# Softmax attention on one core: the bias row built behind the last block's values, three set-up pieces behind the first maxima, and 78 maxima steps ahead of the loop

## The chip, the core and the metric

The kernel runs on one core of a Trainium2 chip, in one launch. A core has five engines that run beside each other and meet at semaphores: TensorE (PE, matrix products and transposes; its weight loads are listed as PEld), VectorE (DVE), ScalarE (ACT), GpSimd (POOL) and SyncE (SP, which here only issues DMAs). The metric is the device time of one execution in microseconds (us); of several runs the median is given.

## The reference, cut to what matters

The input `x` has shape (2, 2048, 256). Four layers follow one another: softmax attention, a gated rotation network ("ffn"), linear attention, and the rotation network again. The change touches the first layer alone:

```python
def _L0_attn_a_ref(x, Wq, bq, Wk, bk, Wv, bv, Wo, bo):   # HIDDEN 256, 16 heads of 16, 4 key/value heads
    q = x @ Wq + bq
    k = x @ Wk + bk
    v = x @ Wv + bv
    ...
    scores = jnp.einsum('bghnd,bhsd->bghns', q, k)
    attn = jax.nn.softmax(scores / SCALE, axis=-1)        # SCALE = 4
    out = jnp.einsum('bghns,bhsd->bghnd', attn, v)
    out = out.transpose(0, 3, 1, 2, 4).reshape(B, N, NUM_HEADS * HEAD_DIM)
    return out @ Wo + bo
...
x = x + _L0_attn_a_ref(_layernorm(x, axis=-1), ...)
x = x + _L0_ffn_ref(_layernorm(x, axis=-1), ...)
x = x + _L0_attn_b_ref(_layernorm(x, axis=-1), ...)
x = x + _L0_ffn_ref(_layernorm(x, axis=-1), ...)
```

## The kernel before, in words

**Blocks and units.** The 4096 tokens are cut into NB = 8 blocks of BLK = 512 tokens, of which blocks 0 to 3 are batch 0 and 4 to 7 batch 1. A *unit* u = (j, g) is one block of queries and one group g of four heads, one for each of the KV = 4 key/value heads r; there are 32 units. Softmax is done with the true maxima, so each score is computed twice: once with queries on the partitions, to find the largest score of each query, and once with keys on the partitions, for the exponentials.

**The maxima.** `largest()` is a generator. One *step* of it is one 128x512 score product `s` on PE (line 376) and one reduction `mx` on DVE (line 380). A unit has 64 steps: 4 blocks of keys, 4 tiles of queries, and the heads r in the order 0, 1, 3, 2. The 16 features of a head are held as high and low parts in 64 rows; head r uses rows 0 to 63 of the array when r is even and rows 64 to 127 when r is odd (`row` in `step`). The products go through a ring of three PSUM banks (`a_s`, tag `s`), so step n cannot write before step n-3 has been reduced. Unit 0 alone also uses banks of the ring `p`. After 64 steps the generator negates and splits the maxima (`nm`, line 390, and `mt`, lines 394 to 398), turns them (`mr`, line 403) and sends them over DRAM to `mrows` (lines 407 and 412). For unit 0 this happens at once; for the units after it the turn is done inside the next unit's first steps, after the step (kb, qi, r) = (0, 0, 2), which is that unit's fourth.

**The first stage.** Before the loop, blocks are normalised (`look`, `spread`), turned (`features`, line 131), and projected to keys (`keys`, 309), queries (`asked`, 336) and values (`values`, 326). What is left of this after the first four steps of the maxima is the generator `pieces()`, 22 pieces long: queries of blocks 1 to 3, then features, keys and two times queries for each of the blocks 4 to 7. The lines 622 to 627 of the kernel before run the steps 4 to 73 (`LEAD` = 74) and put a piece behind certain steps: behind every third one from 4 to 52, then behind 64, 66, 68, 70 and 72. The order of DVE, ACT, POOL and SP in this stage is the order of the program (`in_order`), and PE's is too, up to the first passes of the loop.

**The bias row.** `rows()` is a generator that loads the output weights and the bias `bo` with nine DMAs on SP (lines 216 and 217), multiplies it into a diagonal on POOL (`a_db`, line 221), sums that over partitions with a product on PE (`a_pb`, line 226) and copies the row on DVE (`a_bo_row`, line 227). In the kernel before, POOL's part stands behind the queries of block 3 and ahead of the features of block 4, and the PE and DVE part behind the values of block 4. The row is used first when unit 0 is finished (line 467), in the loop.

**The loop.** There are 32 x 16 = 512 passes, one for each unit u and each 128 keys kb. A pass issues on PE, in this order: two steps of the maxima, `score(0)`, `score(1)`, `shift(0)`, `shift(1)`, `score(2)`, one step, `score(3)`, `shift(2)`, one step, `shift(3)`, and then the four products `av` of the pass before (`weigh`, line 633). `score` is line 648 and `shift`, which adds the negated maxima, line 652; both use rows 0 to 63 for even r and rows 64 to 127 for odd r. ACT takes the exponentials `e` (line 656). In the kernel before, a pass with odd kb among the first twelve (`MORE` = 6) takes one more step at its end. The steps are counted through all units, so that the remainder of the count by four says which heads the steps of a pass belong to; the maxima end 20 passes ahead of the end of the loop.

Of the kernel before, what the change touches and what calls it, by code (L numbers as in the profile page):

```python
# [67 lines left out]
def tile_hybrid(ctx: ExitStack, tc: tile.TileContext, x: bass.AP, consts: bass.AP, wa_d: bass.AP, wf_d: bass.AP, wb_d: bass.AP, out: bass.AP):  # L68
# [84 lines left out]
    def attention_a():  # L153
        with ExitStack() as st:
# [206 lines left out]
            def largest():  # L361


                turning = []
                for u, (j, g) in enumerate(units):
                    k0 = (j // BPB) * N
                    qP = queries[u]
                    mx = sb.tile([P, KV, 4, 4], F32, tag="mx", name=f"mx{u}")
                    first = u == 0

                    def step(kb, qi, r):

                        pool, tag = (psp, "p") if first and (4 * qi + r) % 5 > 2 else (pss, "s")
                        s = pool.tile([P, BLK], F32, tag=tag, name=f"s{u}_{kb}_{qi}_{r}")
                        row = slice(64 * (r % 2), 64 * (r % 2) + 64)
                        mm(  # L376
                            s, qP[r // 2][row, qi * P : (qi + 1) * P],
                            kP[r // 2][row, k0 + kb * BLK : k0 + (kb + 1) * BLK], start=True, stop=True,
                        )
                        nc.vector.tensor_reduce(mx[:, r, qi : qi + 1, kb], s, AX.X, ALU.max)  # L380

                    for kb in range(4):
                        for qi in range(4):
                            for r in (0, 1, 3, 2):
                                step(kb, qi, r)
                                if (kb, qi, r) == (0, 0, 2) and turning:
                                    turning.pop()()
                                yield
                    nm = sb.tile([P, KV, 4], F32, tag="nm", name=f"nm{u}")
                    nc.vector.tensor_reduce(nm, mx, AX.X, ALU.max, negate=True)  # L390

                    mt = sb.tile([P, KV, 2, 4], F32, tag="mt", name=f"mt{u}")
                    if first:
                        nc.vector.tensor_copy(mt[:, :, 0, :].bitcast(F32R), nm)
                        nc.vector.tensor_tensor(mt[:, :, 1, :], nm, mt[:, :, 0, :], ALU.subtract)
                    else:
                        nc.scalar.copy(mt[:, :, 0, :].bitcast(F32R), nm)  # L397
                        nc.gpsimd.tensor_tensor(mt[:, :, 1, :], nm, mt[:, :, 0, :], ALU.subtract)  # L398

                    def turn_maxima(u=u, mt=mt):  # L400

                        mr = sb.tile([P, 32], F32, tag="mr", name=f"mr{u}")
                        turn = nc.vector.transpose(mr, mt.rearrange("p r i q -> p (r i q)"))
                        tc.keep_in_program_order(turn)
                        d = dram.tile([2 * KV, BLK], F32, tag="dm", name=f"dm{u}")
                        for i in range(4):
                            nc.sync.dma_start(
                                d.rearrange("r (q b x) -> (r q) b x", b=4, x=32)[:, i, :], mr[32 * i : 32 * i + 32, :]
                            )
                        for p in range(2):  # L410
                            for i in range(2):
                                nc.sync.dma_start(
                                    mrows[u % 2][p][64 * i : 64 * i + 2, :].bitcast(F32),
                                    d[4 * p + 2 * i : 4 * p + 2 * i + 2, :],
                                )

                    if first or u + 1 == len(units):
                        turn_maxima()
                    else:
                        turning.append(turn_maxima)  # L420
# [83 lines left out]
                        nc.vector.tensor_tensor(pair, pair, po.rearrange("p (t d) -> p t d", t=2), ALU.add)  # L504
                        yield


            LEAD, MORE, WARM = 64 + 10, 6, 6
            ahead = largest()
            begin = len(nc.cur_bb.bb.instructions)  # L510
            loads = ExitStack()
# [81 lines left out]
            def pieces():  # L593

                memsets()
                look(4)
                values(3)
                for j in range(1, BPB):
                    for m in range(2):
                        asked(j, m)  # L600
                        yield
                        if (j, m) == (2, 0):
                            spread(4, ld, 0)
                next(more)
                for j in range(BPB, NB):
                    features(j, ld, 0)
                    if j + 1 < NB:
                        look(j + 1)
                    yield
                    keys(j, ld)()  # L610
                    if j + 1 < NB:
                        spread(j + 1, ld, 0)
                    yield
                    asked(j, 0)
                    yield
                    asked(j, 1)
                    values(j)
                    if j == BPB:
                        next(more)
                    yield  # L620

            rest = pieces()
            for n in range(4, LEAD):
                next(ahead)
                if (n % 3 == 1 and n < 55) or (n > 63 and n % 2 == 0):
                    next(rest, None)
            in_order(begin, (engines.DVE, engines.Activation, engines.Pool, engines.SP))

# [9 lines left out]
            for u, kb in ((u, kb) for u in range(len(units)) for kb in range(KB)):  # L638
                if (u, kb) == (0, 4):
                    in_order(begin, (engines.PE,))  # L640
                qP, mrow = queries[u], mrows[u % 2]
                k0 = units[u][0] // BPB * N + kb * P
                t, es = [], []

                def score(r):
                    row = slice(64 * (r % 2), 64 * (r % 2) + 64)
                    t.append(psp.tile([P, BLK], F32, tag="p", name=f"p{u}_{kb}_{r}"))
                    mm(t[r], kP[r // 2][row, k0 : k0 + P], qP[r // 2][row, :], start=True, stop=False)  # L648

                def shift(r):  # L650
                    row = slice(64 * (r % 2), 64 * (r % 2) + 64)
                    mm(t[r], pick[row, :], mrow[r // 2][row, :], start=False, stop=True)  # L652

                def exp(r):
                    es.append(sb.tile([P, BLK], F32, tag="e", name=f"e{u}_{kb}_{r}", bufs=8))
                    nc.scalar.activation(es[r], t[r], AF.Exp, scale=1.0 / HD**0.5)  # L656


                next(ahead, None)
                next(ahead, None)  # L660
                score(0)
                score(1)
                shift(0)
                shift(1)
                exp(0)
                exp(1)
                if kb == 1:
                    next(done, None)
                score(2)
                next(ahead, None)  # L670
                score(3)
                shift(2)
                next(ahead, None)
                shift(3)
                exp(2)
                exp(3)
                if last is not None:
                    if last[1] == 0:
                        av = pav.tile([P, BLK], F32, tag="av", name=f"av{last[0]}")
                    weigh(*last)  # L680
                    if last[1] == KB - 1:
                        done = finish(last[0], av)
                last = u, kb, es
                if kb > 1:
                    next(done, None)
                    next(norms, None)
                if kb % 2 == 1 and u * KB + kb < 2 * MORE:
                    next(ahead)
                if u % G == 1 and kb == 1 and G < u < 4 * G:
                    norms = norm(u // G - 1)  # L690
                if kb == 4 and u + 2 < len(units):
                    project(u + 2)()
                if rest is not None and next(rest, "end") == "end":
                    rest = None
                    loads.close()
                    late = later_pools["late"] = ctx.enter_context(tc.tile_pool(name="late", bufs=1, side="right"))
                    for n, (name, of) in enumerate((("wf", wf_d), ("wb", wb_d))):
                        weights[name] = late.tile([P, of.shape[1]], F32, name=name)
                        nc.sync.dma_start(weights[name], of)
                    for name in ("w4", "b3"):  # L700
                        at = slice(*_WF[name])
                        nc.sync.dma_start(weights["wf"][64:P, at], wf_d[0:64, at])
# [826 lines left out]
```

## Time and profile before

| What | Value |
|---|---|
| Time, median of 3 runs | 2137.04 us (2135.6 to 2137.55) |
| The profiled execution | 2140.99 us, span 2139.2 us |
| PE busy | 2109.2 us (99%) |
| DVE busy | 1701.3 us (80%) |
| ACT busy | 1428.9 us (67%) |
| POOL busy | 355.6 us (17%) |
| Mean granted PE clock | 0.990 |
| `mx` on DVE, 2048 times | 1272.2 us, mean 683 ns |
| `e` on ACT, 2048 times | 1057.7 us, mean 603 ns |
| First score of the loop on PE | 106.78 us |
| Last step of the maxima begins on PE | 1481.31 us |

The span is the time from the first to the last instruction of the core; the execution's own time lies 1.8 us above it. Busy PE time holds matrix products that overlap: two products in different halves of the rows run beside each other, and the mean of one (471 ns for `s`) contains its latency. Idle time of an engine is put down to the instruction that released it. The granted clock is what the throttle let through to PE, 1.00 or 0.50 in every row of this profile that lies between two changes.

### The profile page before, as it was taken

What the parts mean: (1) busy time and instruction counts of PE and PEld (TensorE: products, weight loads), DVE (VectorE), ACT (ScalarE), POOL (GpSimd) and SP (SyncE); (2) the same over time, 40 slices, a digit from 0 to 9 for tenths busy, and PEclk for the clock granted to TensorE, in tenths of its full rate; (3) what the DMA queues carried; (4) which work ended last, traced back from release to release, by engine and by line L of the source; (5) the groups of instructions that cost most, each with busy time, mean ns of one, the idle gap of its engine ahead of it and who ended that gap; (6) DMA issues with size and microseconds to landing.
All of it is one profiled execution on the core that took longest, in us unless ns stands there. A gap on an engine that the chain in (4) does not pass through costs nothing.

```text
span 2139.2 us, 38744 instructions
## 1 busy us (share of the span) xinstructions
PE 2109.2 (99%) x14158; PEld 1018.1 (48%) x14158; DVE 1701.3 (80%) x3241; ACT 1428.9 (67%) x2787; POOL 355.6 (17%) x352
## 2 busy tenths in 40 slices
PE   9899999999999999999999999999999999999998
PEld 4344444444444444444444444444443567676434
DVE  7699998998998999899899899986134688876335
ACT  4377777776777877777777777778864445454443
POOL 3100000000001000000000000000145345541450
PEclk9799999999999999999999999999999999999999
DMA  6320110101101011010110101100100000000002
GB/s 207 88 87 10 49 37 17 47 10 47 39 17 37 19 47 39 17 48 10 46 39 17 44 12 47 39 17 8 52 0 1 1 1 1 2 1 2 0 0 79
DMA packets 59695, 68.71 MB, mean 32 GB/s; under 512 B 24944, under 2 KB 34032, under 8 KB 59248
## 3 DMA queue, kind: packets, MB, share of 16 engines
q1 hardware_dynamic: 58592, 64.79, 11.1%
q8 instruction: 111, 1.82, 0.3%
q10 hardware_dynamic: 720, 0.92, 0.1%
q14 instruction: 80, 0.66, 0.1%
q0 software_dynamic: 192, 0.52, 0.1%
HBM read 35.78 MB, written 26.21 MB: 29 GB/s over the span
## 4 chain that ended last, share of the span: by engine, by line
PE 93%; DVE 3%; issue 1%; ACT 1%; POOL 1%; DMA 1%; SPq 0%; DVEq 0%; POOLq 0%; ACTq 0%
PE av L633 24%; PE s L376 22%; PE p L648 11%; PE q1f L817 8%; PE p L652 7%; PE q2f L827 4%; PE pe L1114 2%; PE bpo L1140 1%; PE po L499 1%; PE pq L975 1%; PE pv L984 1%; PE pw L984 1%; PE pk L975 1%; PE q3f L839 1%; DVE mx L380 1%
## 5 line engine op out<-in xcount | busy, mean ns | idle before, releaser
L380 DVE TENSOR_REDUCE mx<-s 128x1 f32<-128x512 f32 x2048 | 1272.2, 683 | 111.9 <-PE s L376 106.2
L656 ACT ACTIVATE e<-p 128x512 f32<-128x512 f32 x2048 | 1057.7, 603 | 313.5 <-PE p L652 306.5
L376 PE MATMUL s<-a_kP,qP 64*128 64x512 f32 x2048 | 707.0, 471 | 4.9 <-DVE mx L380 3.0
L652 PE MATMUL p<-a_m,a_pick 64*128 64x512 f32 x2048 | 587.4, 415 | 0.0
L376 PEld LDWEIGHTS s<-a_kP,qP 64*128 64x128 f32 x2048 | 283.6, 184 | 569.6 <-DVE mx L380 553.1
L633 PE MATMUL av<-e,a_v 128*32 128x512 f32 x4096 | 546.8, 605 | 0.0
L648 PE MATMUL p<-qP,a_kP 64*128 64x512 f32 x2048 | 526.7, 394 | 2.6 <-ACT e L656 2.6
L648 PEld LDWEIGHTS p<-qP,a_kP 64*128 64x128 f32 x2048 | 286.9, 185 | 64.2 <-ACT e L656 25.4
L652 PEld LDWEIGHTS p<-a_m,a_pick 64*128 64x128 f32 x2048 | 284.2, 184 | 26.3
L817 PE MATMUL q1f<-zq,wf 128*128 128x512 f32 x384 | 175.6, 600 | 0.0
L633 PEld LDWEIGHTS av<-e,a_v 128*32 128x32 f32 x4096 | 81.0, 108 | 129.6 <-issue 121.5
L818 ACT ACTIVATE a1f<-q1f,wf 128x512 f32<-128x512 f32 x96 | 65.8, 686 | 102.8 <-PE q1f L817 99.4
L398 POOL TENSOR_TENSOR mt<-nm,mt 128x16 f32<-128x16 f32 x31 | 6.9, 221 | 737.3 <-ACT mt L397 737.3
L817 PEld LDWEIGHTS q1f<-zq,wf 128*128 128x128 f32 x384 | 70.5, 190 | 97.5 <-issue 85.5
L827 PE MATMUL q2f<-a1f,wf 128*128 128x512 f32 x192 | 89.8, 610 | 0.0
L1120 DVE TENSOR_TENSOR en<-pe,small 128x512 f32<-128x512 f32 x128 | 79.3, 682 | 12.8 <-PE pe L1114 12.6
L237 POOL TENSOR_TENSOR ql<-zq,qh 128x512 f32<-128x512 f32 x15 | 19.3, 1286 | 359.6 <-ACT qh L234 359.6
L858 DVE TENSOR_SCALAR cf<-cf,f_beta,alphaf 128x512 f32<-128x512 f32 x32 | 33.6, 1051 | 54.0 <-ACT cf L857 53.8
L862 POOL TENSOR_TENSOR tf<-cf,zq 128x512 f32<-128x512 f32 x32 | 56.6, 1769 | 92.2 <-DVE cf L858 91.8
L829 ACT ACTIVATE a2f<-q2f,wf 128x512 f32<-128x512 f32 x48 | 32.6, 685 | 52.4 <-PE q2f L827 52.4
L864 POOL TENSOR_TENSOR zq<-zq,tf 128x512 f32<-128x512 f32 x32 | 56.8, 1776 | 2.5
L827 PEld LDWEIGHTS q2f<-a1f,wf 128*128 128x128 f32 x192 | 35.2, 193 | 45.3 <-issue 44.1
(209 smaller groups left out, 1636.1 us busy)
## 6 DMA issues: line engine op xcount, KB each, us to landing
qP<-dq SPq DMA_DIRECT2D x64, 256.0 KB
dq<-qh SPq DMA_DIRECT2D x62, 128.0 KB
dq<-ql SPq DMA_DIRECT2D x62, 128.0 KB
a_kP<-dk SPq DMA_DIRECT2D x16, 256.0 KB
oc<-avs SPq DMA_DIRECT2D x128, 32.0 KB
sums<-dr SPq DMA_DIRECT2D x128, 32.0 KB
out<-xs SPq DMA_DIRECT2D x16, 256.0 KB
xs<-in_x SPq DMA_DIRECT2D x7, 512.0 KB
```

What stands on the lines that cost most here:

```text
L376: mm(s, qP[r // 2][row, qi * P : (qi + 1) * P], kP[r // 2][row, k0 + kb * BLK : k0 + (kb + 1) * BLK], start=True, stop=True,)
L380: nc.vector.tensor_reduce(mx[:, r, qi : qi + 1, kb], s, AX.X, ALU.max)
L633: mm(av[32 * r : 32 * r + 32, :], vA[:, units[u][0] // BPB * KB + kb, 32 * r : 32 * r + 32], es[r], start=(kb == 0), stop=(kb == KB - 1),)
L648: mm(t[r], kP[r // 2][row, k0 : k0 + P], qP[r // 2][row, :], start=True, stop=False)
L652: mm(t[r], pick[row, :], mrow[r // 2][row, :], start=False, stop=True)
L656: nc.scalar.activation(es[r], t[r], AF.Exp, scale=1.0 / HD**0.5)
L817: mm(q1, w1[:, c, m * P : (m + 1) * P], z[:, c, :], start=(c == 0), stop=(c == 1))
L818: nc.scalar.activation(a1[:, m, :], q1, AF.Gelu, bias=b1[:, m : m + 1])
L827: mm(q2, w2[:, c, :], a1[:, c, :], start=(c == 0), stop=(c == 1))
L862: nc.gpsimd.tensor_tensor(t1, cs, z[:, 0, :], ALU.mult)
L864: nc.gpsimd.tensor_tensor(z[:, 1, :], z[:, 1, :], t1, ALU.subtract)
L1120: nc.vector.tensor_tensor(self.ens[t][w], pes[w].rearrange("p (h n) -> p h n", h=4), const("triu").unsqueeze(1).to_broadcast([P, 4, P]), A ...
```

## The change

The turn of each unit's maxima moves from the step (0, 0, 2) to (0, 0, 3), which is the third step of a unit. The constant `MORE` and the extra steps of the loop go, and `LEAD` rises from 74 to 78. The bias row's parts on POOL, PE and DVE move together behind the values of block 7. The pieces now stand behind every third step from 4 to 58 and behind the steps 64, 66 and 69; there are 22 as before. The DMAs of `rows()` stay where they were.

```diff
@@ largest()
-                                if (kb, qi, r) == (0, 0, 2) and turning:
+                                if (kb, qi, r) == (0, 0, 3) and turning:
                                     turning.pop()()
@@ first stage
-            LEAD, MORE, WARM = 64 + 10, 6, 6
+            LEAD, WARM = 64 + 14, 6
@@ pieces()
-                next(more)
                 for j in range(BPB, NB):
                     features(j, ld, 0)
...
                     asked(j, 1)
                     values(j)
-                    if j == BPB:
+                    if j + 1 == NB:
+                        next(more)
                         next(more)
                     yield
@@ the steps ahead of the loop
             for n in range(4, LEAD):
                 next(ahead)
-                if (n % 3 == 1 and n < 55) or (n > 63 and n % 2 == 0):
+                if n % 3 == 1 and n < 61 or n in (64, 66, 69):
                     next(rest, None)
@@ the loop
                 if kb > 1:
                     next(done, None)
                     next(norms, None)
-                if kb % 2 == 1 and u * KB + kb < 2 * MORE:
-                    next(ahead)
```

## The prediction

> **What bounds the kernel now.** I read the page first, then the chain of waits of the first stage, then PE's stretches by granted clock, and last PE's order of time inside single passes of the loop.
>
> ```profile
> span 2139.2 us, 38744 instructions
> ...
> PE 93%; DVE 3%; issue 1%; ACT 1%; POOL 1%; DMA 1%; SPq 0%; DVEq 0%; POOLq 0%; ACTq 0%
> ```
>
> The chain that ended last is PE for 93% of the span: a slot added to PE's order in the loop is paid in full, and DVE or ACT work there is paid only where PE waits for it. The first stage is different. Stretches (PE busy, PEld, DVE, ACT, POOL, then the granted clock):
>
> ```profile
> 56.81:60.23 3.42, 0.06 (x1) 0.06 (x1) 0.00 (x0) 0.00 (x0) 0.87 (x3) 1.00 0.44 89
> 60.23:70.47 10.24, 8.82 (x20) 4.24 (x20) 6.03 (x17) 4.65 (x9) 3.48 (x5) 0.50 0.31 83
> ...
> 84.12:87.53 3.41, 1.60 (x5) 0.55 (x4) 3.41 (x6) 0.00 (x0) 0.00 (x0) 1.00 0.52 110
> 87.53:101.19 13.66, 13.50 (x28) 6.05 (x28) 7.03 (x15) 2.19 (x5) 0.00 (x0) 0.50 0.13 41
> ```
>
> PE stands still once, then runs 10.24 us at half clock; later a stretch of steps at DVE's pace is followed by 13.66 us at half clock. The first hole is the bias row, in the chain of waits:
>
> ```profile
> 59.36 0.75 POOL a_db L221 x2
> ...
> 64.10 1.97 PE tr L131 x8
> ...
> 76.82 1.03 PE tr L131 x8
> ```
>
> `a_db` waits until 59.36 for `bo`, the last of nine DMAs that SP issues from 52.71 on; PE's `a_pb` waits for `a_db` (4.26 us idle), and so do POOL's scales of block 5 and ACT's normalisation behind them, for which the transposes `tr` wait (1.42 us).
>
> In the loop I compare passes by the start of `av` in the chain. The count of steps at a pass's start, by four, is its *phase*: 74 + 4 kb + kb/2 (rounded down) in unit 0.
>
> ```profile
> 127.29 1.00 PE av L633 x8
> 129.99 1.00 PE av L633 x8
> 133.53 0.99 PE av L633 x8
> 136.46 1.00 PE av L633 x8
> ```
>
> From 127.29 to 129.99 is pass 7 (count 105, phase 1): 2.70. From 133.53 to 136.46 is pass 9 (count 114, phase 2): 2.93. Neither holds an extra step. The others likewise: passes 5 and 13 (phase 0) 2.70 and 2.71, passes 3 and 11 (phase 3) 2.92 and 2.93. Why, is seen in the second halves of pass 9 and of pass 13, PE's timeline:
>
> ```profile
> 135.25 0.39 PE L648 MATMUL p<-qP,a_kP 64*128 64x512 f32 x2
> 135.48 0.39 PE L376 MATMUL s<-a_kP,qP 64*128 64x512 f32 x1
> 135.72 0.39 PE L652 MATMUL p<-a_m,a_pick 64*128 64x512 f32 x1
> 135.73 0.50 PE L376 MATMUL s<-a_kP,qP 64*128 64x512 f32 x1
> 136.07 0.39 PE L652 MATMUL p<-a_m,a_pick 64*128 64x512 f32 x1
> 136.39 0.64 PE L633 MATMUL av<-e,a_v 128*32 128x512 f32 x4
> ```
>
> ```profile
> 150.65 0.39 PE L376 MATMUL s<-a_kP,qP 64*128 64x512 f32 x1
> 150.65 0.62 PE L648 MATMUL p<-qP,a_kP 64*128 64x512 f32 x2
> 150.88 0.38 PE L652 MATMUL p<-a_m,a_pick 64*128 64x512 f32 x1
> 151.13 0.49 PE L376 MATMUL s<-a_kP,qP 64*128 64x512 f32 x1
> 151.13 0.50 PE L652 MATMUL p<-a_m,a_pick 64*128 64x512 f32 x1
> 151.56 0.64 PE L633 MATMUL av<-e,a_v 128*32 128x512 f32 x4
> ```
>
> The pass's last step stands ahead of `shift(3)`, which uses the upper rows. In phase 0 that step is head 2 (lower rows) and both start at 151.13. In phase 2 it is head 1 (upper rows): `shift(3)` follows it 0.34 later, and `av` starts 1.94 after the pass's start (134.45) against 1.71 (149.85). The step itself stands 1.28 after the pass's start in both, held by the ring of three: the pass's first product takes 0.50 and its reduction 0.60. Cheap phases are thus 0 and 1 (last head 2 or 0), dear ones 2 and 3 (last head 1 or 3).
>
> **The change part by part.** All sums are against the profiled 2139.2; the execution took 2140.99, 4 above the runs' median, so I take differences from the trace and put them on 2137.0.
>
> *Phase of the loop.* Before, 74 and six extra steps reach 80, a multiple of four, after pass 11: of the 492 passes with steps 484 are cheap and 8 dear. After, 78 leaves the remainder 2 and no extra step mends it; a unit has 64 steps, so it stays. In the changed order the step ahead of `shift(3)` is head 1 in all 492. Price: 2.93 - 2.705 = 0.225 for each of 484 passes, **+108.9**. Bounds: 0.20 to 0.24 by the spread of those passes, +97 to +116. Passes that already wait for ACT or DVE swallow some of it: the units with normalisations last 47.4 and 48.8 against 43.3, about 7 of it waits; I take **-2** (0 to -7).
>
> *Six extra steps removed from the loop.* Passes behind an extra step took 3.31 and 3.30 in phases 0 and 1, 3.53 in 2 and 3: 0.60 each, one DVE reduction. **-3.6.**
>
> *Bias row moved.* At 55.91 PE goes straight on to three steps and block 5's `tr`, at about 56.6 and not 64.10: -7.5. From that `tr` to the next took 12.7 at half clock (64.10 to 76.82); a warm block needs 9.85 (query products of block 5 at 71.35, of block 6 at 81.20): -2.8. Together **-10.3**; the low end is the idle time alone, -5.7. In the new place `bo` landed long ago; `a_db` (0.75) follows `kl` of block 7 on POOL while PE has two query products of 1.91 to do, so nothing waits, and nothing that PE needs is queued behind it on POOL. `a_pb` costs 0.6 and the DVE copy 0.42 wherever they stand. The SP queue keeps its order, but block 4's key DMAs are no longer late behind POOL; they are first read by unit 16.
>
> *Pieces and 78 steps.* In before's time, with a warm clock: DVE is busy without a break from 76.39; the query products behind step 55 delay it by 0.65, so unit 0's last reduction ends at 91.3 (before: 90.6). PE then needs, from 90.3 on, keys 1.9, queries twice 1.9, values 0.3, `a_pb` 0.6 and six steps between, to 98.1. The last eight steps and the loop's first two run at 0.604 each (14 took 8.45), three of them at once for the ring: the first score at 103.1, before 106.78. **-3.7**, with four steps more done. The maxima of unit 0 landed at 96.25 and were first used at 107.0; 10.8 of slack cover the 0.7.
>
> *Clock at the end of the stage.* The stretch at DVE's pace between `a_pb` and the loop, about 5 us, has half-row products alone. The row 84.12 to 87.53 is like it: PE busy 1.60 of 3.41, and the clock fell. The Trainium skill ("TensorE: Matmul & The Clock Gate", "Why this matters for your kernels") asks only that PE have no idle gap over about 3 us; the gaps here are under 0.5 us, so by the rule this part costs 0 and the sum is 2 lower. The row decides: the stretches at half clock last multiples of 3.41 (10.24, 13.66); two of these, about 4.4 us of them in the loop, cost **+2.2**. Bounds 0 and +7 (another fall between steps 58 and 64, as in before's 13.66 us).
>
> *Turn and end.* `nm` comes half a pass later, and the turn a step later, than before. The maxima rows were issued 4 us or more ahead of their use in most units, 2 in the tightest (1314.68, used 1316.72), and land 0.75 after the issue; half a pass is 1.4, and the passes are longer. 0, at worst +1 in a few units, which I count as part of the range. Two steps move into the pass of unit 30 that had none: **+0.3**.
>
> Sum: 108.9 - 2 - 3.6 - 10.3 - 3.7 + 2.2 + 0.3 = +91.8, so **2229 us**.
>
> **The rivals.** (a) *The phase costs nothing*, and the kernel ends at 2137 - 17 = 2120, faster. That needs the last step of a pass to start one slot (0.25) earlier, beside the other half's step, at 135.48 in the lines above; its bank is free only after 0.50 + 0.60 of product and reduction, and longer passes don't shorten these. If it starts by 1.03 after the pass's start the cost is gone; by 1.28 it is whole. (b) *Half of it is hidden*: longer passes let waits for ACT and for weight loads shrink (`s` loads wait 520 us in sum for `mx`, beside `av`). Then some 0.11 for each pass, 2175. Against it: passes 3, 9 and 11 already ran with DVE idle before them and show no such gain. (c) *A new wait for the maxima*: the rows come late in each unit by up to 1.4, 30 units, 2229 + 30 to 40 = 2265. The slack of 1.3 to 3.3 speaks against it.
>
> **How the numbers follow.** Main case 0.91, (a) 0.03, (b) 0.03, (c) 0.03. Within the main case the pass price gives -12 and +7, the first stage -2 and +9: 2215 to 2240 holds about 85 of its 91, and (b), (c) and (a) lie outside. 0.2% is what a measurement of this kernel can tell from no change, 4 us: slower 0.96, faster 0.03, same 0.01.
>
> **What would show it.** Right: passes of 2.93 all through the loop (46.9 for a plain unit, before 43.3), `shift(3)` 0.34 behind the last step, PE still the chain; the first score near 93; no idle hole at 56 to 60; half clock, if at all, around the loop's start. Wrong: plain units of 43.3, or PE waiting for `a_m`, or half clock from 76 to 90 again.

## The result and the profile after

The changed kernel takes 2231.34 us (median of 5 runs, 2231.3 to 2235.15) against 2137.55 us of the kernel before (5 runs); the ratio is 1.044, with a 95% interval of 1.0427 to 1.0453. It is slower by 94 us; the prediction said 92. The profiled execution has a span of 2233.4 us, 94.2 above that of the kernel before.

The page of the changed kernel, its span and the chain that ended last by engine:

```profile
span 2233.4 us, 38741 instructions
...
PE 96%; DVE 2%; ACT 1%; DMA 1%; POOL 1%; issue 0%; SPq 0%; DVEq 0%; ACTq 0%; POOLq 0%
```

PE's share of the chain rose from 93% to 96%: there is more of PE's order to go through, and less of anything else. The chain of waits of the first stage:

```profile
58.49 1.02 PE tr L131 x8
...
68.59 1.02 PE tr L131 x8
...
78.59 1.02 PE tr L131 x8
...
89.02 0.63 PE a_pb L226 x2
```

The hole is gone. The transposes of blocks 5, 6 and 7 follow each other at 10.1 and 10.0 us with the clock at 1.00, and `a_pb` comes behind the values of block 7 without a wait. The stretches of PE show the same, and the fall of the clock (PE busy, PEld, DVE, ACT, POOL, granted clock):

```profile
53.40:56.81 3.41, 3.41 (x10) 1.35 (x9) 3.41 (x7) 2.52 (x5) 1.26 (x1) 1.00 0.59 199
90.05:93.46 3.41, 2.46 (x8) 0.91 (x5) 3.40 (x7) 0.00 (x0) 0.00 (x0) 1.00 0.59 126
93.46:100.29 6.83, 6.48 (x25) 4.23 (x24) 5.24 (x10) 3.05 (x6) 0.00 (x0) 0.50 0.87 287
```

In the loop the chain's `av` groups stand 2.93 apart, in these first passes and in those of unit 20 (1010.52 to 1013.45) alike:

```profile
103.48 1.00 PE av L632 x8
106.40 1.00 PE av L632 x8
```

And one pass of unit 2 in PE's timeline has the form of pass 9 before:

```profile
204.11 0.50 PE L376 MATMUL s<-a_kP,qP 64*128 64x512 f32 x2
...
204.91 0.39 PE L647 MATMUL p<-qP,a_kP 64*128 64x512 f32 x2
205.15 0.39 PE L376 MATMUL s<-a_kP,qP 64*128 64x512 f32 x1
205.38 0.39 PE L651 MATMUL p<-a_m,a_pick 64*128 64x512 f32 x1
205.39 0.50 PE L376 MATMUL s<-a_kP,qP 64*128 64x512 f32 x1
205.73 0.39 PE L651 MATMUL p<-a_m,a_pick 64*128 64x512 f32 x1
206.05 0.64 PE L632 MATMUL av<-e,a_v 128*32 128x512 f32 x4
```

The last step stands 1.28 behind the pass's start (205.39), `shift(3)` 0.34 behind it (205.73), and `av` 1.94 behind the start. The reduction that frees the last step's bank is that of the pass's first product, in DVE's timeline:

```profile
204.65 0.69 DVE L380 TENSOR_REDUCE mx<-s 128x1 f32<-128x512 f32 x1 [0.45 <-PE s L376]
```

It begins 0.54 behind the product and takes 0.69; the last step begins 0.05 after its end. Where the 94.2 us are, by marks that both traces have:

| Stretch | before | after | difference |
|---|---|---|---|
| start to the loop's first score | 106.78 | 94.46 | -12.3 |
| first score to `nm` of unit 1 | 38.80 | 38.18 | -0.6 |
| `nm` of unit 1 to `nm` of unit 31 (480 passes) | 1337.50 | 1444.73 | +107.2 |
| `nm` of unit 31 to the end | 656.1 | 656.0 | -0.1 |

A plain unit, the commonest, with nothing in it but its 16 passes, went from 43.3 to 46.93 (from one `nm` to the next): 0.227 for each pass.

### The profile page after: what moved, and what is told of

Its sections match the earlier page's. It is cut to its first block, busy times and chain, and to the rows that moved or that the text cites. A ratio compares the mean times of both kernels' runs of the same rounds, so it can differ in the third digit from the quotient of the medians.

```text
span 2233.4 us, 38741 instructions
## 1 busy us (share of the span) xinstructions
PE 2210.6 (99%) x14158; PEld 1155.0 (52%) x14158; DVE 1701.8 (76%) x3241; ACT 1429.9 (64%) x2787; POOL 355.4 (16%) x352
## 4 chain that ended last, share of the span: by engine, by line
PE 96%; DVE 2%; ACT 1%; DMA 1%; POOL 1%; issue 0%; SPq 0%; DVEq 0%; ACTq 0%; POOLq 0%
PE av L632 23%; PE s L376 18%; PE p L651 16%; PE p L647 11%; PE q1f L814 7%; PE q2f L824 4%; PE pe L1111 2%; PE bpo L1137 1%; PE po L499 1%; PE pq L972 1%; PE pw L981 1%; PE pk L972 1%; PE pv L981 1%; PE pq L336 1%; PE q3f L836 1%; PE b_sums L1153 1%
## 5 line engine op out<-in xcount | busy, mean ns | idle before, releaser
L376 PE MATMUL s<-a_kP,qP 64*128 64x512 f32 x2048 | 638.0, 470 | 3.1 <-DVE mx L380 1.5
L647 PE MATMUL p<-qP,a_kP 64*128 64x512 f32 x2048 | 416.7, 394 | 1.2 <-ACT e L655 0.9
L647 PEld LDWEIGHTS p<-qP,a_kP 64*128 64x128 f32 x2048 | 201.3, 185 | 45.2 <-ACT e L655 23.9
```

Source lines behind the costliest of these rows:

```text
L376: mm(s, qP[r // 2][row, qi * P : (qi + 1) * P], kP[r // 2][row, k0 + kb * BLK : k0 + (kb + 1) * BLK], start=True, stop=True,)
```

## The experiments

Two accounts fit the result of the changed kernel alone: that the remainder of 78 by four puts the last step of a pass into the half of the rows that `shift(3)` needs (theory T), or that the loop lost its extra steps and gets its maxima half a pass later (rival M). A third, S, takes PE's products to start strictly in their order, so that both inner steps of a pass count.

### 80 steps ahead

```diff
-            LEAD, WARM = 64 + 14, 6
+            LEAD, WARM = 64 + 16, 6
```

> The changed kernel with 80 steps ahead of the loop, a multiple of four; nothing else. Theory T (the last step of a pass shares its half of the rows with shift(3) in the remainders 2 and 3, and av is pushed back by 0.228): all 492 passes cheap, plain units 43.3 us as in the kernel before; the first stage gains some 14, the six extra steps 3.6, two more steps ahead of the loop cost 1.2: 2118 to 2123. Rival M (the loss is the lost extra steps and the maxima that come half a pass later, not the remainder): about 2230. Rival S (PE starts its products strictly in order, so both inner steps count): as T, cheap.

Measured: 2121.01 us (2117.27 to 2123.2), 0.9926 of the kernel before (0.9911 to 0.9941). Plain units take 43.3. Two steps more ahead of the loop take 110 us off the changed kernel. M, which had about 2230, falls here: there are still no extra steps in the loop. (The maxima come half a pass earlier than with 78; the run with other heads holds that fixed.) PE's timeline of a pass:

```profile
194.56 0.62 PE L647 MATMUL p<-qP,a_kP 64*128 64x512 f32 x2
194.79 0.38 PE L651 MATMUL p<-a_m,a_pick 64*128 64x512 f32 x1
195.04 0.49 PE L376 MATMUL s<-a_kP,qP 64*128 64x512 f32 x1
195.04 0.50 PE L651 MATMUL p<-a_m,a_pick 64*128 64x512 f32 x1
195.47 1.07 PE L632 MATMUL av<-e,a_v 128*32 128x512 f32 x8
```

The last step and `shift(3)` start together at 195.04, 1.28 behind the pass's start (193.76), and `av` follows 0.43 later.

### 77 and 79 steps ahead

```diff
-            LEAD, WARM = 64 + 14, 6
+            LEAD, WARM = 64 + 13, 6     # the second kernel: 64 + 15
```

> The changed kernel with 77 steps ahead, remainder 1: the last step of a pass is head 0 (lower rows), but the two steps that open a pass are heads 1 and 3, both in the upper rows. T: the opening pair costs nothing that shows, plain units 43.3, 2118 to 2123. S: one slot more in each pass, as in the changed kernel, about 2229. M: about 2231.

> The changed kernel with 79 steps ahead, remainder 3: the last step is head 3 (upper rows), and the inner pair is 1 and 3, the opening pair 2 and 0. T: dear like remainder 2, plain units 46.9, 2229 to 2233. S: two slots in each pass, plain units 50.6, about 2340. M: about 2231.

Measured: 2119.65 us with 77 (2115.99 to 2120.14; ratio 0.9917, 0.9903 to 0.9932) and 2232.51 us with 79 (2231.03 to 2233.17; 1.045, 1.0433 to 1.0468). Both are where T has them. S is 110 us off in each: it made 77 dear and 79 twice as dear as 78. With 77 steps the pass opens with two steps of the upper rows, and nothing is lost:

```profile
204.19 0.49 PE L376 MATMUL s<-a_kP,qP 64*128 64x512 f32 x1
204.19 0.49 PE L647 MATMUL p<-qP,a_kP 64*128 64x512 f32 x1
204.52 0.38 PE L376 MATMUL s<-a_kP,qP 64*128 64x512 f32 x1
204.53 0.39 PE L651 MATMUL p<-a_m,a_pick 64*128 64x512 f32 x1
204.74 0.40 PE L647 MATMUL p<-qP,a_kP 64*128 64x512 f32 x2
...
205.46 0.50 PE L376 MATMUL s<-a_kP,qP 64*128 64x512 f32 x1
205.47 0.49 PE L651 MATMUL p<-a_m,a_pick 64*128 64x512 f32 x1
205.89 1.06 PE L632 MATMUL av<-e,a_v 128*32 128x512 f32 x8
```

The two opening steps start at 204.19 and 204.52, the second behind the first in the same rows. In the other half, `score(0)` starts at 204.19 and `shift(0)` at 204.53, beside the second step and 0.21 ahead of `score(1)` (204.74), which stands before `shift(0)` in the source and in the program built from it. Each half of the rows keeps its own order here; across the halves these starts do not. (The profiler models the ends of products, so only starts are compared.) The Trainium skill ("TensorE: Matmul & The Clock Gate", "The mechanism") says that matmuls keep the program's order in start and end, "strict FIFO, no reordering"; these starts differ, and by that rule, as S works it out, 77 steps would have been as dear as 78.

### 78 steps, other heads

```diff
-                            for r in (0, 1, 3, 2):
+                            for r in (3, 2, 0, 1):
                                 step(kb, qi, r)
-                                if (kb, qi, r) == (0, 0, 3) and turning:
+                                if (kb, qi, r) == (0, 0, 0) and turning:
```

> The changed kernel with 78 steps ahead as it is, but with the heads of a step in the order 3, 2, 0, 1 in place of 0, 1, 3, 2 (the turn stays at a unit's third step). Counts, pieces and maxima come when they came; only which half of the rows a step uses is different: the last step of a pass is head 2. T: cheap, plain units 43.3, 2117 to 2122. S: cheap too. M: about 2231, since nothing of the timing of maxima or extra steps is changed.

Measured: 2124.15 us (2123.55 to 2125.29; 0.9943, 0.9928 to 0.9958), plain units 43.2. Every count and the place of every turn is that of the changed kernel; in the loop only the half of the rows that a step uses differs, and the 107 us are gone. The time is 2 above the range that was given: the loop is as short as with 80 steps (1371.2 against 1371.7 from the first score to `nm` of unit 31), and the first score comes at 97.1 against 93.5. Two things differ in this first stage: the profiled execution has 3.41 us of half clock from 27.63 on, and unit 0 chooses its ring by the head (`(4 * qi + r) % 5 > 2`), so its banks come in another order. How much each makes is not shown.

### The last step behind `shift(3)`

```diff
                 shift(2)
-                next(ahead, None)
                 shift(3)
+                next(ahead, None)
```

> The changed kernel, 78 steps ahead and heads as they are, with two instructions of a pass exchanged: the last step is issued behind shift(3) and not ahead of it. T: shift(3) has its half of the rows free at once, the step starts 1.28 after the pass's start as before and av follows 0.43 later: plain units 43.3 to 43.9, 2118 to 2128. If it is not this neighbourhood but the heads of the pass as a whole (rival H): plain units stay at 46.9, about 2231.

Measured: 2120.33 us (2119.47 to 2121.78; 0.9918, 0.9903 to 0.9933), plain units 43.2. The exchange of two neighbours in PE's order, with the heads and the 78 steps as they are, takes the whole cost away; rival H falls. PE's timeline:

```profile
210.22 0.50 PE L376 MATMUL s<-a_kP,qP 64*128 64x512 f32 x2
...
211.26 0.38 PE L651 MATMUL p<-a_m,a_pick 64*128 64x512 f32 x1
211.26 0.39 PE L376 MATMUL s<-a_kP,qP 64*128 64x512 f32 x1
211.50 0.39 PE L651 MATMUL p<-a_m,a_pick 64*128 64x512 f32 x1
211.50 0.49 PE L376 MATMUL s<-a_kP,qP 64*128 64x512 f32 x1
211.93 1.06 PE L632 MATMUL av<-e,a_v 128*32 128x512 f32 x8
```

`shift(3)` now starts at 211.26, as soon as its rows are free, and the last step at 211.50, still 1.28 behind the pass's start; `av` comes 1.71 behind it.

### The kernel before with four extra steps

```diff
-            LEAD, MORE, WARM = 64 + 10, 6, 6
+            LEAD, MORE, WARM = 64 + 10, 4, 6
```

> The kernel before with four extra steps in the loop and not six, so that the count reaches 78 and stays at remainder 2 from the eighth pass on; nothing of the first stage is changed. T: 480 passes dear by 0.228, two extra steps of 0.6 fewer: 2137 + 109 - 1 = 2243 to 2248. M (extra steps matter by their number): 2137 to 2142.

Measured: 2245.08 us (2244.78 to 2249.21; 1.0505, 1.0488 to 1.0523), plain units 46.93. The old kernel with its first stage untouched and two steps fewer in its loop is 109 us slower than the kernel before (2136.16 in the runs beside it); M falls here too. It is the remainder that the six extra steps mend, and not what each of them does.

### The bias row alone

```diff
-                next(more)
                 for j in range(BPB, NB):
...
-                    if j == BPB:
+                    if j + 1 == NB:
+                        next(more)
                         next(more)
```

> The kernel before with the bias row behind the values of block 7, and nothing else. The first hole and its half-clock stretch go: -10.3 by the prediction, between -5.7 (the idle time alone) and -12; the run of steps without pieces and its fall of the clock stay: about 2127. If the time there is taken up by the later stretch at DVE's pace: 2133 to 2137.

Measured: 2126.1 us (2124.09 to 2130.61; 0.9954, 0.9935 to 0.9973), 10.1 below the kernel before (2136.16 in the runs beside it). Its chain of waits:

```profile
56.74 1.02 PE tr L131 x8
66.82 1.02 PE tr L131 x8
83.89 1.02 PE tr L131 x8
```

Blocks 5 and 6 come at 56.7 and 66.8, where before had 64.1 and 76.8: 7.4 and 10.0 earlier. Block 7 still waits behind the run of steps without pieces. A fall of the clock stays there too, but a shorter one (columns as above):

```profile
72.97:76.38 3.41, 3.17 (x10) 1.32 (x9) 3.41 (x7) 1.15 (x3) 0.63 (x1) 1.00 0.93 257
76.38:83.20 6.82, 5.52 (x14) 2.22 (x12) 5.61 (x13) 0.37 (x1) 0.00 (x0) 0.50 0.38 104
```

The half clock here lasts 6.82, where the trace of before has 13.66, and the first score comes at 93.94 against 106.78. The length of that stretch differs without this change as well: the kernel with four extra steps has the first stage of before, and in its trace the stretch lasts 6.83 and the first score comes at 105.09.

### 80 steps, the last pieces later

```diff
-            LEAD, WARM = 64 + 14, 6
+            LEAD, WARM = 64 + 16, 6
...
-                if n % 3 == 1 and n < 61 or n in (64, 66, 69):
+                if n % 3 == 1 and n < 61 or n in (64, 68, 73):
```

> The changed kernel with 80 steps ahead and the last three pieces behind the steps 64, 68 and 73 in place of 64, 66 and 69, so that fewer steps at DVE's pace stand alone ahead of the loop. If the fall of the clock at the loop's start costs the 2.2 of the prediction: 2 below the kernel with 80 steps and the pieces where they were, and no stretch at half clock between 85 and 105. If the fall is not set by this stretch: the same time as that kernel, clock low again for 6.8.

Measured: 2122.82 us (2121.42 to 2124.04; 0.9929, 0.9913 to 0.9944), not below the 2121.01 of 80 steps with the pieces where they were. The fall of the clock is gone in the profiled execution, as the stretch of this kernel shows:

```profile
85.00:105.00 20.00, 18.21 (x97) 7.88 (x95) 16.70 (x29) 9.51 (x19) 0.00 (x0) 1.00 0.48 152
```

But the first score comes at 94.56 and not 93.52, and `nm` of unit 1 at 126.97 and not 126.40. Between these two marks 0.5 is gained, and ahead of them 1.0 is lost. That the place of the pieces took the fall away is not shown: it is one profiled execution of each kernel, and with the pieces where they were the stretch ahead of the fall (at 89.63) is not one of half-row products alone, since it holds `a_pb`, which uses all rows, at 86.83 and 87.15:

```profile
86.22:89.63 3.41, 2.76 (x12) 1.28 (x11) 2.06 (x4) 0.95 (x2) 0.00 (x0) 1.00 0.70 150
```

The mean clocks of the four runs are 0.995 to 0.997 here and 0.994 to 0.997 there. What the runs do show is that moving the pieces gains nothing.

### Half of each reduction

```diff
-                        nc.vector.tensor_reduce(mx[:, r, qi : qi + 1, kb], s, AX.X, ALU.max)
+                        nc.vector.tensor_reduce(mx[:, r, qi : qi + 1, kb], s[:, 0 : BLK // 2], AX.X, ALU.max)
```

Both kernels leave out half of the maxima's work on DVE. The first has 78 steps ahead, the second 80 (`LEAD` = 64 + 16).

> The changed kernel, 78 steps ahead, with each reduction of a step over the first 256 of the 512 scores alone: half of the maxima's work on DVE is left out. The bank of a pass's first product comes free some 0.27 earlier, so that its last step can start by 1.03 after the pass's start and not at 1.28. T with rival (a)'s condition (the cost comes from a last step that is held by the ring and stands ahead of shift(3) in the same half): the pass falls back to 2.70 or 2.71, plain units 43.3, and with a shorter first stage (about 90 steps at 0.33 in place of 0.60, partly behind PE) 2100 to 2118. Rival (d) (products of one half of the rows ahead of shift(3) cost a slot whenever they come): plain units stay at 46.9, 2212 to 2228.

> The same half of the reductions left out, with 80 steps ahead: the control. T: in remainder 0 PE's order fills the pass whether the last step is held or not, plain units 43.2 to 43.3, 2100 to 2118, and within 5 of the kernel with 78 steps and half reductions. If plain units fall well below 43 here, DVE's hold was part of the cheap pass too.

Measured: 2106.29 us with 78 (2102.76 to 2107.73; 0.9852, 0.9835 to 0.9868), plain units 42.67; 2059.01 us with 80 (2058.29 to 2061.96; 0.9635, 0.9621 to 0.965), plain units 41.5. The first is in its range of time (its units are shorter than the 43.3 that was given), and rival (d) falls; the control is not in its range: the two were to lie within 5 of each other and lie 47 apart. PE's timelines, with 78 steps:

```profile
200.35 0.49 PE L376 MATMUL s<-a_kP,qP 64*128 64x512 f32 x2
...
201.38 0.48 PE L376 MATMUL s<-a_kP,qP 64*128 64x512 f32 x2
201.62 0.47 PE L651 MATMUL p<-a_m,a_pick 64*128 64x512 f32 x2
202.02 1.06 PE L632 MATMUL av<-e,a_v 128*32 128x512 f32 x8
```

and with 80:

```profile
201.37 0.49 PE L376 MATMUL s<-a_kP,qP 64*128 64x512 f32 x2
...
202.63 0.39 PE L376 MATMUL s<-a_kP,qP 64*128 64x512 f32 x1
202.65 0.39 PE L651 MATMUL p<-a_m,a_pick 64*128 64x512 f32 x1
202.97 1.06 PE L632 MATMUL av<-e,a_v 128*32 128x512 f32 x8
```

With 78 steps and short reductions the last step starts 1.03 behind the pass's start, beside the inner step of the other half: this is the point from which the prediction's rival (a) was to decide. The pass falls from 2.93 to 2.67. With 80 it falls too, from 2.705 to 2.59, all of it between the last group's start and `av`: 0.32 and not 0.43. So the ring's hold makes at least 0.15 of the 0.227 between the two remainders, and takes 0.11 of the cheap pass besides; 0.07 between the remainders stays.

Where these 0.07 lie, the traces show. With 78 steps, DVE's reduction of the pass's first product, the weight load of the last step, and `shift(3)`, which the timeline above merges with `shift(2)`:

```profile
200.88 0.42 DVE L380 TENSOR_REDUCE mx<-s 128x1 f32<-128x256 f32 x1 [0.98 <-PE s L376]
201.36 0.18 PEld L376 LDWEIGHTS s<-a_kP,qP 64*128 64x128 f32 x1
201.70 0.39 PE L651 MATMUL p<-a_m,a_pick 64*128 64x512 f32 x1
```

and with 80 the weight load of the last step:

```profile
202.40 0.18 PEld L376 LDWEIGHTS s<-a_kP,qP 64*128 64x128 f32 x1
```

With 80 the weights are loaded 0.22 before the step starts (202.63). With 78 they are loaded only when the reduction has ended (201.31), 0.02 before the step starts (201.38), and `shift(3)` stands 0.32 behind the step, as it does in the changed kernel (0.34), 0.08 later than `shift(2)` (201.62). From `shift(3)` to `av` it is 0.32 in both. So with 78 the last step was still held, only for less long. The same is seen in the cheap pass: with 80 steps and whole reductions the last step's weights are loaded at 195.04, as the step starts. That a still shorter reduction would take the 0.07 away was not run.

### 76 steps, and a bank moved to the ring of the steps

```diff
-            LEAD, WARM = 64 + 14, 6
+            LEAD, WARM = 64 + 12, 6
```

> The changed kernel with 76 steps ahead, remainder 0 again and four steps fewer than with 80: a step costs 0.60 ahead of the loop where DVE sets the pace and about 0.1 in it, so the start comes 2 earlier; the maxima of each unit come one pass (2.7) later, and with 77 steps their rows landed 1.6 to 1.8 ahead of their use, with 80 some 3.4. If that slack is enough: 2116 to 2120, the best of all. If PE comes to wait for the rows in many units: plain units above 43.5 and 2122 to 2140.

Measured: 2121.85 us (2116.93 to 2124.29; 0.9922, 0.99 to 0.9945), plain units 43.3. No wait for the maxima, and no gain over 77 or 80 either.

```diff
-            LEAD, WARM = 64 + 14, 6
+            LEAD, WARM = 64 + 16, 6
...
-            pss = st.enter_context(tc.tile_pool(name="a_s", bufs=3, space=PSUM))
-            psp = st.enter_context(tc.tile_pool(name="a_p", bufs=4, space=PSUM))
+            pss = st.enter_context(tc.tile_pool(name="a_s", bufs=4, space=PSUM))
+            psp = st.enter_context(tc.tile_pool(name="a_p", bufs=3, space=PSUM))
```

> The changed kernel with 80 steps ahead, and one of the eight PSUM banks moved from the ring of the scores p (four to three) to the ring of the steps s (three to four), so that a pass's last step waits for the reduction of the step four before it and not three; nothing is left out. If the hold of the last step goes and p gets by with three banks: passes of 2.59 to 2.62, plain units near 41.6, 2060 to 2085, better than all. If score(3) now waits for the exponential of score(0), whose bank it takes (ACT takes 0.55 for one, and starts only behind shift(0)): about 0.5 a pass more than 2.70, plain units 48 to 52, 2220 to 2400.

Measured: 2473.72 us (2472.97 to 2476.1; 1.1569, 1.155 to 1.1589), plain units 53.7, past even the dear end that was given. PE's timeline of a pass (idle time and its releaser in brackets):

```profile
221.82 0.39 PE L647 MATMUL p<-qP,a_kP 64*128 64x512 f32 x1
...
222.73 0.50 PE L647 MATMUL p<-qP,a_kP 64*128 64x512 f32 x1 [0.29 <-ACT e L655]
```

`score(3)` starts 0.91 behind `score(2)`, waiting for the exponential that frees its bank. With three banks the scores hold PE; the 62 us between 2121 and 2059 cannot be had this way.

## Why the prediction was right

**The phase of the loop.** Predicted +108.9 with 2 swallowed, 480 of the passes making 106.0 of it. Measured from `nm` of unit 1 to `nm` of unit 31: +107.2. A pass costs 0.227 more, the price taken from pass 9 of the trace of before was 0.225. The runs with 77, 79 and 80 steps, with other heads, and with two instructions exchanged leave none of the named rivals: times fall into two groups, 2120 to 2124 and 2231 to 2233, by whether the step ahead of `shift(3)` uses its half of the rows. The 2 that were to be swallowed are not seen. One of the long units that the prediction read as waits (48.8) holds a stretch at half clock, which the trace after has not there:

```profile
514.21:517.61 3.40, 3.40 (x18) 1.17 (x16) 1.36 (x3) 1.93 (x4) 0.00 (x0) 0.50 0.52 154
```

The same unit takes 47.3 in the kernel with the bias row alone. Without these 1.5 the difference is 108.7, or 0.226 for each of the 480 passes, and nothing is left that was swallowed.

**The mechanism.** The prediction had the last step held by the ring at 1.28, and `shift(3)` stuck behind it in the same rows. Both parts are shown: with the step behind `shift(3)` the cost is gone, and with a shorter reduction the step starts at 1.03 and most of it goes. Two terms were mis-sized. The hold was put at 0.50 for the product and 0.60 for the reduction, which makes 1.10 and not 1.28: 0.60 is the distance from one reduction to the next, and the first of a pass takes 0.69, from 0.54 behind the product on. And the cost was to be gone altogether with a start at 1.03; 0.07 of 0.227 stayed against the control, where the traces show the step's weights still loaded late.

**The bias row.** Predicted -10.3; alone it gave -10.1, within an interval of -14 to -6. The gain at the transposes of block 6 is the forecast one (10.0). Behind them the later half clock was shorter in the profiled execution, which was not forecast; that the total agrees as well as it does is in part luck.

**The first stage.** Predicted -14.0 to the first score, measured -12.3. The profiled execution after has 3.41 us of half clock at 11.54 that before has not; the transposes of block 4 begin at 48.4 against 46.3, 2.1 later. From there to the first score it is 46.1 against 60.5, -14.4. The kernel with two instructions exchanged has the same first stage without that stretch, and its first score comes at 92.53, -14.3; against the 105.09 of the kernel with four extra steps it is -12.6. So the sum holds to some 2 us, which is what the clock moves from one execution to the next. The split does not hold: the bias row alone brought the first score to 93.94, and the pieces and the four steps, put at -3.7, took only another 1.4 off.

**The extra steps** were put at -3.6 and were not run alone. Between the first score and `nm` of unit 1 the two traces differ by -0.6: -3.6 for the steps, +0.9 for the four passes there that turned dear, +1.4 for `nm` half a pass later leaves 0.7 for the clock. The kept traces allow an estimate of the steps: between these marks the kernel with the bias row alone takes 38.68, those with 80 steps 32.88 and 32.41; less 1.8 for eight passes that are dear in the first only, the six steps are worth 4.0 to 4.5, and the clock 1.0 to 1.5.

**The clock at the end of the stage.** It fell, at 93.46 and for 6.83, two times 3.41, as forecast. The rule of the Trainium skill ("TensorE: Matmul & The Clock Gate", "Why this matters for your kernels") that the prediction quotes, no idle gap over about 3 us, would have had it stay: PE was busy 2.46 of the 3.41 before the fall, with no idle time over 0.54. In the row of before from which the fall was forecast one gap is longer than the prediction says: 1.29 us, up to 87.69, not under 0.5. The price was put at +2.2; by the lines above it is 0.7 to 1.5 behind the first score, and what it cost ahead of it is not separated.

**The maxima.** No pass waits for them. The last load of a unit's rows is issued 4.0 ahead of their use in the median unit (before 4.2), 1.9 in the tightest (before 2.0). The end after `nm` of unit 31 did not move (-0.1).

**The sum.** That 92 and 94 lie so near is better than the terms deserve. The two profiled executions lie some 4 us above the medians of their kernels, and stretches at half clock that only one of them has moved their first stages by about 2 us. The term that decides, 109 in a sum of 94, is shown by experiments.

## What to carry to other kernels

Where PE runs two half-row products side by side, the count of instructions put ahead of a loop decides by its remainder which halves meet in each pass, and one slot of 0.227 us (the distance of two products in the same half) in each of 484 passes (110 us) outweighs the 12.3 us that this first stage gained. Before a count is changed, write out which half each product of one pass uses and which of them starts late because of a ring; a dear remainder is mended here by two steps more, by another order of the heads, or by issuing the late step last. That turns the same change from +94 us into some -16 (2119.65 to 2121.85 with 76, 77 or 80 steps, or with 78 and the step behind `shift(3)`: these cannot be told apart).

## What the runs showed that was not expected

- DVE is busy 80% of the span before, and PE is busy 99%; yet a reduction shorter by half takes 62 us off the kernel with 80 steps (2121.01 to 2059.01), 58 of it between the first score and `nm` of unit 31. In the pass the gain lies behind the last step: its weights are loaded ahead of time, and `av` follows 0.32 behind `shift(3)` and not 0.43. How long a single reduction keeps its bank costs time here, though DVE has idle time in each pass.
- Two products in different halves of the rows start in another order than the program's (204.53 ahead of `score(1)` with 77 steps), while those of one half keep theirs.
- A bank taken from the scores costs 353 us (2473.72 against 2121.01), although ACT is busy only 64% of the changed kernel's span.
- PE's clock also falls where PE does not stand still: in the 3.41 us before a fall PE was busy 2.46 in the changed kernel, 2.76 with 80 steps and 3.17 with the bias row alone. The half clock then lasts a multiple of 3.41 us: 6.83 in these three and 13.66 in the kernel before; the 10.24 there followed a standstill of PE. What decides a fall is open.
